# The end of the last block of a gated cross-attention: where x is added, and how the root mean square is formed

## The chip, the cores and the metric

The kernel runs on one core of a Trainium2 chip. A core has a matrix engine (TensorE, PE in the profile, with its weight loads shown apart as PEld), VectorE (DVE), ScalarE (ACT), GpSimd (POOL) and an engine that here only issues transfers (SyncE, SP). Each works through its own list of instructions in order, and they wait for each other by semaphores. Sixteen DMA engines move data between the memory of the chip (HBM) and the core's memory (SBUF). TensorE writes into banks of a small memory of its own, PSUM, which VectorE and ScalarE read.

The metric is the time of one execution in microseconds on the device. The kernel before took 1021.86 us, the median of three runs between 1018.0 and 1022.25.

## The reference

```python
memory_proj = jnp.einsum('bme,de->bmd', memory, W_mem)
scores = jnp.einsum('bnd,bmd->bnm', hidden_states, memory_proj) / jnp.sqrt(jnp.float32(D))
attn = jax.nn.softmax(scores, axis=-1)
memory_context = jnp.einsum('bnm,bmd->bnd', attn, memory_proj)
gate_input = jnp.concatenate([hidden_states, memory_context], axis=-1)
gate = jax.nn.sigmoid(jnp.einsum('bnf,df->bnd', gate_input, W_gate) + b_gate)
fused = hidden_states + gate * memory_context
return _rmsnorm(fused, norm_w)     # x * rsqrt(mean(x*x, -1) + 1e-6) * w
```

Here hidden_states is x, of shape (8, 1024, 1024); memory is (8, 64, 512); the gate has D = 1024 columns. All is in 32-bit floats.

## The kernel before, in words

The 8192 rows of x are worked in 16 blocks of 512 rows, called quads (`q`), two for each batch entry. A quad has four tiles of 128 rows (`t` = 0 to 3); tiles 0 and 1 are row 0 of a two by two scheme, tiles 2 and 3 are row 1. The columns are worked in two halves of 512 (`h`).

The product of x with the upper half of W_gate is made by a fast matrix multiplication in two levels. On the outer level a quad needs seven products, in the order 1, 6, 7, 5, 4, 2, 3 (`ORDER`). Each is again made of seven small ones, which `outer_product` writes in the order A, B, C, D, A (a second part, summed onto the first in the same bank), E, F: two matmuls of 256 columns each. GpSimd forms the sums of x that serve as left operands (`inner_s`), one product ahead. The results are joined by VectorE and GpSimd: ScalarE copies the first part of A (`u<-kA`, line 589) and must have done so before TensorE sums the second part of A onto it; VectorE forms u2, u3, u4 from it with B, C and D; GpSimd adds these to the sums of earlier products (`pre`); VectorE then adds A, D, E and F into the tiles `gate` (`fin`).

Products 5, 4, 2 and 3 each complete a half of two tiles: 5 the second half of row 1, 4 the first half of row 1, 2 the first half of row 0, 3 the second half of row 0. In these (they have an entry `ext` in `ORDER`) TensorE also multiplies the attention weights with the projected memory: once into banks of the gate, once into `pc`, the memory context itself (two buffers, used in turn). ScalarE then takes the sigmoid of the half (line 489), and VectorE multiplies it with `pc` (`gated`, lines 483 to 485). A tile's gating frees its buffer `pc`, which TensorE needs in the next product.

After product 4 (for row 1) and product 3 (for row 0) follow, for each tile:

- `residual` (line 493): a DMA issued by GpSimd that adds x from HBM onto the tile in SBUF,
- `square` (line 503): ScalarE squares the tile, 1024 columns at once, and sums them,
- the root, for two tiles at once (line 508); it needs another table of functions than the sigmoid, loaded by an instruction of its own (ACT_TABLE_LOAD),
- `norm` (lines 514 and 518): VectorE forms the reciprocal and multiplies each half by it and by the weights,
- a store of the whole tile, 512 KB, issued by SP (line 96).

The order is written out by hand. A counter, `slot`, advances with each small product, and `at(slot, f)` puts the instructions of `f` ahead of that small product; `mid` puts them beside the additions of one product. What falls due behind the last product is written out in order of its slots. In most quads squares and norms are spread over the next quad's products; in the last one the norms of row 0 have slots 7 to 10 behind product 3, and those of row 1 keep their usual distance, so that most of row 1's norms are written behind those of row 0. Within an engine instructions keep the order in which they are written. SP's list holds loads and stores alike, so a store that waits for its norm holds what is behind it.

x for a quad's left operands is loaded one quad ahead, in chunks, into four buffers `xqpool`, from which VectorE transposes it (line 267). In the last quad nothing is loaded ahead.

Of the kernel before, what the change touches and what calls it, by code (L numbers as in the profile page):

```python
# [20 lines left out]
def tile_gated_cross_attention_rmsnorm(  # L21
# [70 lines left out]
    def tt(eng, o, a, b, op):  # L92
        pin(eng.tensor_tensor(o, a, b, op))  # L93

    def load(o, i):
        pin(nc.sync.dma_start(o, i))
# [4 lines left out]
    def t4k(pool, shape, tag, name):  # L101
        return pool.tile(shape, F32, tag=tag, name=name)
# [145 lines left out]
    def where(q, t=0):  # L248
        return q // QPB, (q % QPB) * QT + t * P
# [183 lines left out]
    def at(slot, fn, *args):  # L433
        due.setdefault(slot, []).append(lambda: fn(*args))
# [8 lines left out]
    def plan(q):  # L443
        t0 = SLOTS * q
        nxt = q + 1 < NQ
        order = [o for o, _ in ORDER]
        for i, o in enumerate(order):
            for part, t in ((0, 1), (1, 5)):
                if i + 1 < len(order):
                    at(t0 + 7 * i + t, inner_s, q, order[i + 1], part)  # L450
                elif nxt:
                    at(t0 + 7 * i + t, inner_s, q + 1, order[0], part)
        at(t0 + 7, scores, q)
        at(t0 + 7, outer_s, q, 3)
        at(t0 + 7, outer_s, q, 4)
        at(t0 + 9, transpose_scores, q)
        at(t0 + 10, softmax_a, q)
        at(t0 + 13, softmax_b, q)
        at(t0 + 17, transpose_attn, q)
        at(t0 + 20, attn_difference, q)  # L460
        if not nxt:
            return
        for i, t in ((2, 0), (3, 1), (4, 2), (5, 3)):
            at(t0 + i, load_xq, q + 1, t)
        for t in (2, 3):
            mid((q, 5), transpose_x, q + 1, t, 0)
            mid((q, 2), transpose_x, q + 1, t, 1)
        for i, t, half in ((36, 0, 0), (38, 1, 0), (43, 0, 1), (45, 1, 1)):
            at(t0 + i, transpose_x, q + 1, t, half)
        mid((q, 3), outer_s, q + 1, 1)  # L470
        mid((q, 3), outer_s, q + 1, 2)
        if (q + 1) % QPB == 0:
            at(t0 + 10, load_mp, (q + 1) // QPB)
            at(t0 + 49, load_mg, (q + 1) // QPB)
# [35 lines left out]
    def norm(q, t, h):  # L510
        b, n0 = where(q, t)
        rstd = rst[q, t // 2]
        if t % 2 == 0 and h == 0:
            pin(nc.vector.reciprocal(rstd, rstd))
        g = O[q, t]
        cols = slice(h * H, (h + 1) * H)
        pin(
            nc.vector.scalar_tensor_tensor(  # L518
                g[:, cols],
                g[:, cols],  # L520
                rstd[:, t % 2 : t % 2 + 1],
                nw_sb[:, cols],
                ALU.mult,
                ALU.mult,
            )
        )
        if h == 1:
            load(out[b, n0 : n0 + P, :], g)
            del O[q, t]

    def outer_product(q, o, ext):

        nonlocal slot, banks
        l11, l12, l21, l22 = quarters(left(q, o))
        s1, s2, s3, s4 = (L2[q, o][:, i, :, :] for i in range(4))
        w = ws[o]
        kb = {}

        def product(name, tag, lhsT, s, start=True):
            nonlocal slot  # L540
            step()
            if name not in kb:
                kb[name] = ps.tile([P, C], F32, tag=banks[tag], name=f"k{name}{q}_{o}")
            for k in range(2):
                mm(kb[name], lhsT[:, k, :], w[:, s, k, :], start and k == 0, k == 1)
            slot += 1

        def o_blocks(row, h):

            for t in (2 * row, 2 * row + 1):  # L550
                if (q, t) not in O:
                    O[q, t] = t4k(gpool, [P, D], "gate", f"gate{q}_{t}")
            return [
                O[q, 2 * row + r][:, h * H + n * C : h * H + (n + 1) * C]
                for r in range(2)
                for n in range(2)
            ]


        sums = {  # L560
            1: [(o_blocks(0, 0), None)],
            6: [(o_blocks(0, 1), (0, 0))],
            7: [(o_blocks(1, 0), (0, 1))] if o == 7 else [],
            5: [(o_blocks(1, 1), (1, 0)), (o_blocks(0, 1), (0, 1))] if o == 5 else [],
            4: [(o_blocks(1, 0), (1, 0))] if o == 4 else [],
            2: [(o_blocks(0, 0), (0, 0))] if o == 2 else [],
            3: [(o_blocks(0, 1), (0, 1))] if o == 3 else [],
        }[o]
        sums = [(dst, src and o_blocks(*src)) for dst, src in sums]

        def pre(n, u):

            for dst, src in sums:
                if src is not None:
                    tt(nc.gpsimd, dst[n], src[n], u, ALU.add)

        def fin(n, name, u):
            for dst, src in sums:
                if src is not None:
                    tt(nc.vector, dst[n], (src if u is None else dst)[n], kb[name], ALU.add)  # L580
                elif u is not None:
                    tt(nc.vector, dst[n], u, kb[name], ALU.add)
                else:
                    pin(nc.scalar.copy(dst[n], kb[name]))

        ut = t4k(rot, [P, 4, C], "u", f"u{q}_{o}")
        p1, u2, u3, u4 = (ut[:, i, :] for i in range(4))
        product("A", 0, l11, R11)
        pin(nc.scalar.copy(p1, kb["A"]))
        product("B", 1, s2, T2)  # L590
        tt(nc.vector, u2, p1, kb["B"], ALU.add)
        product("C", 2, s3, R12)
        tt(nc.vector, u3, u2, kb["C"], ALU.add)
        pre(3, u3)
        pre(2, u3)
        product("D", 3, s1, T1)
        tt(nc.vector, u4, u2, kb["D"], ALU.add)
        pre(1, u4)
        product("A", 0, l12, R21, False)
        pcs = []  # L600
        if ext:
            row, h, g = ext
            at_, mg = attnTs[q], mgs[q // QPB]
            for n in ("E", "F"):
                kb[n] = ps.tile([P, C], F32, tag=banks[4 if n == "E" else 1], name=f"k{n}{q}_{o}")
            for r, names in ((0, ("A", "F")), (1, ("E", "D"))):
                pc = ps_ctx.tile([P, H], F32, tag="ctx", name=f"pc{q}_{o}_{r}")
                for n in range(2):
                    cols = slice(h * H + n * C, h * H + (n + 1) * C)
                    mm(  # L610
                        pc[:, n * C : (n + 1) * C],
                        at_[0:M, 2 * row + r, :],
                        mg[0:M, cols],
                        n == 0,
                        True,
                    )
                    mm(
                        kb[names[n]],
                        at_[M:P, g + r, :],
                        mg[M:P, cols],  # L620
                        names[n] in "EF",
                        True,
                    )
                pcs.append(pc)
        for fn in beside.pop((q, o), ()):
            fn()
        fin(0, "A", None)
        fin(3, "D", u3)
        product("E", 4, l22, T4, not ext)
        fin(2, "E", u3)  # L630
        if ext:
            sigmoid(q, 2 * row + 1, h)
            at(slot + 1, gated, q, 2 * row + 1, h, pcs[1])
        product("F", 1, s4, R22, not ext)
        fin(1, "F", u4)
        if ext:
            sigmoid(q, 2 * row, h)
            at(slot + 2, gated, q, 2 * row, h, pcs[0])
        if o in (4, 3):

            row = ext[0]
            c, d = 2 * row, 2 * row + 1
            for t in (d, c):
                at(slot + 5, residual, q, t)
            if q + 1 == NQ and row == 0:
                when = (7, 8, 9, 9, 10, 10)
            elif row == 0:
                when = (17, 18, 23, 29, None, None)
            else:
                when = (17, 18, 23, 25, 26, 28)  # L650
            at(slot + when[0], square, q, c)
            at(slot + when[1], square, q, d)
            for w_, (t, h_) in zip(when[2:], ((c, 0), (c, 1), (d, 0), (d, 1))):
                if w_ is None:
                    mid((q + 1, 4), norm, q, t, h_)
                else:
                    at(slot + w_, norm, q, t, h_)
        banks = [banks[i] for i in (2, 3, 0, 4, 1)]
        del L2[q, o]
# [34 lines left out]
```

## Time and profile before

| What | Value |
|---|---|
| median of three runs | 1021.86 us |
| profiled execution | 1022.17 us |
| its span, first to last instruction | 1020.4 us |
| granted TensorE clock, mean | 0.986 |
| TensorE busy | 982.8 us, 96% of the span |
| VectorE busy | 752.8 us, 74% |
| GpSimd busy | 690.5 us, 68% |
| ScalarE busy | 320.2 us, 31% |
| stores `out<-gate`, 64 of 512 KB | 2.6 us from issue to landing (median) |
| `gate<-in_x`, 64 of 512 KB | 7.4 us from issue to landing (median) |

A profile is of one execution. Times in it count from its first instruction. A group row gives the line of the code, engine, operation, output and inputs, their shapes and the count, then busy time in us and the mean in ns, then the idle time ahead of it and what ended most of that. A timeline row gives start and duration in us, and in brackets the idle time before and its releaser. The chain is followed back from the end: at each step to what released it.

### The profile page before, as it was taken

What the parts mean: (1) busy time and instruction counts of PE and PEld (TensorE: products, weight loads), DVE (VectorE), ACT (ScalarE), POOL (GpSimd) and SP (SyncE); (2) the same over time, 40 slices, a digit from 0 to 9 for tenths busy, and PEclk for the clock granted to TensorE, in tenths of its full rate; (3) what the DMA queues carried; (4) which work ended last, traced back from release to release, by engine and by line L of the source; (5) the groups of instructions that cost most, each with busy time, mean ns of one, the idle gap of its engine ahead of it and who ended that gap; (6) DMA issues with size and microseconds to landing.
All of it is one profiled execution on the core that took longest, in us unless ns stands there. A gap on an engine that the chain in (4) does not pass through costs nothing.

```text
span 1020.4 us, 14598 instructions
## 1 busy us (share of the span) xinstructions
PE 982.8 (96%) x4976; PEld 767.9 (75%) x4976; DVE 752.8 (74%) x1464; ACT 320.2 (31%) x587; POOL 690.5 (68%) x855
## 2 busy tenths in 40 slices
PE   7898999999999999999999999999999999999991
PEld 4443687888888887888788888888888878878881
DVE  2065667878878787878787787878787878878763
ACT  0200023334241523333243425142333334341512
POOL 0000477877878787878788787878787878878671
PEclk9899999999999999999999999999999999999996
DMA  7675608164643727192825455372718271543324
GB/s 246 185 187 152 169 1 171 68 140 108 153 106 83 186 76 162 63 187 83 166 73 132 117 131 128 81 188 69 170 62 184 86 165 70 125 128 83 84 72 134
DMA packets 75945, 126.78 MB, mean 124 GB/s; under 512 B 16224, under 2 KB 53088, under 8 KB 75872
## 3 DMA queue, kind: packets, MB, share of 16 engines
q1 hardware_dynamic: 64160, 86.01, 29.0%
q0 software_dynamic: 9216, 33.56, 17.9%
q10 hardware_dynamic: 2496, 6.29, 2.1%
q8 instruction: 39, 0.64, 0.3%
q14 instruction: 34, 0.28, 0.1%
HBM read 85.98 MB, written 39.85 MB: 123 GB/s over the span
## 4 chain that ended last, share of the span: by engine, by line
PE 82%; DVE 12%; DMA 3%; issue 1%; SPq 1%; ACT 0%; ACTq 0%; DVEq 0%; POOL 0%
PE kA L90 17%; PE pc L90 12%; PE kE L90 10%; PE kD L90 8%; PE kF L90 8%; PE kB L90 8%; PE kC L90 7%; PE psT L90 6%; DVE gate L518 5%; PE pm L90 3%; PE pg L90 3%; DVE gate L93 2%; DVE e L93 2%; DVE u L93 1%; DMA gate<-in_x 1%
## 5 line engine op out<-in xcount | busy, mean ns | idle before, releaser
L93 POOL TENSOR_TENSOR gate<-gate,u 128x256 f32<-128x256 f32 x336 | 269.1, 830 | 116.1 <-DVE u L93 92.8
L93 POOL TENSOR_TENSOR l<-a 128x256 f32<-128x256 f32 x128 | 125.5, 980 | 168.3 <-DVE a L267 104.8
L489 ACT ACTIVATE gate<-gate 128x512 f32<-128x512 f32 x128 | 79.3, 630 | 412.1 <-DVE gate L93 412.1
L90 PE MATMUL kA<-ws,a 128*128 128x256 f32 x512 | 131.5, 379 | 0.0
L90 PE MATMUL pc<-mg,attnT 64*128 64x256 f32 x512 | 127.4, 389 | 0.0
L518 DVE SCALAR_TENSOR_TENSOR gate<-gate,ss,nw_sb 128x512 f32<-128x512 f32 x128 | 121.6, 963 | 1.1
L90 PE MATMUL kC<-ws,l 128*128 128x256 f32 x448 | 115.1, 379 | 0.8 <-DVE g L93 0.8
L90 PE MATMUL kD<-ws,l 128*128 128x256 f32 x448 | 115.0, 379 | 0.0
L90 PE MATMUL kB<-ws,l 128*128 128x256 f32 x448 | 115.0, 379 | 0.0
L90 PE MATMUL kF<-ws,l 128*128 128x256 f32 x448 | 115.0, 379 | 0.0
L90 PEld LDWEIGHTS pc<-mg,attnT 64*128 64x128 f32 x512 | 90.6, 186 | 29.8 <-issue 21.2
L90 PEld LDWEIGHTS kA<-ws,a 128*128 128x128 f32 x512 | 97.2, 190 | 13.8 <-DVE s L93 0.2
L90 PE MATMUL kA<-ws,s 128*128 128x256 f32 x384 | 100.2, 383 | 0.0
L90 PEld LDWEIGHTS kB<-ws,l 128*128 128x128 f32 x448 | 85.1, 190 | 11.6
L90 PEld LDWEIGHTS kF<-ws,l 128*128 128x128 f32 x448 | 85.1, 190 | 11.6
L90 PEld LDWEIGHTS kC<-ws,l 128*128 128x128 f32 x448 | 83.8, 190 | 11.8 <-POOL l L93 1.1
L90 PEld LDWEIGHTS kD<-ws,l 128*128 128x128 f32 x448 | 83.9, 190 | 10.7
L93 DVE TENSOR_TENSOR gate<-gate,pc 128x512 f32<-128x512 f32 x128 | 87.1, 681 | 5.3 <-ACT gate L489 5.1
L267 DVE STREAM_TRANSPOSE a<-xq 128x512 f32<-128x512 f32 x128 | 86.0, 693 | 0.0
L93 POOL TENSOR_TENSOR l<-s 128x256 f32<-128x256 f32 x96 | 77.6, 809 | 8.4 <-PE kF L90 5.8
L90 PEld LDWEIGHTS kA<-ws,s 128*128 128x128 f32 x384 | 71.6, 190 | 15.2 <-DVE a L93 6.2
L93 DVE TENSOR_TENSOR u<-u,kB 128x256 f32<-128x256 f32 x112 | 46.8, 418 | 46.3 <-PE kB L90 41.6
(84 smaller groups left out, 1688.0 us busy)
## 6 DMA issues: line engine op xcount, KB each, us to landing
xq<-in_x SPq DMA_DIRECT2D x256, 128.0 KB, 5.5
gate<-in_x POOLq DMA_DIRECT2D x64, 512.0 KB, 7.4
out<-gate SPq DMA_DIRECT2D x64, 512.0 KB, 2.6
w<-in_w_gate_t SPq DMA_DIRECT2D x32, 128.0 KB, 3.3
ws<-in_w_gate_t SPq DMA_DIRECT2D x32, 128.0 KB, 2.9
mg<-mgd SPq DMA_DIRECT2D x8, 512.0 KB, 3.6
wm<-in_w_mem_t SPq DMA_DIRECT2D x4, 512.0 KB, 6.8
mgd<-mp ACTq DMA_DIRECT2D x8, 256.0 KB, 4.4
```

What stands on the lines that cost most here:

```text
L90: pin(nc.tensor.matmul(o, lhsT, rhs, start=start, stop=stop, skip_group_check=True))
L93: pin(eng.tensor_tensor(o, a, b, op))
L267: nc.vector.transpose(A[key][:, :, r * P : (r + 1) * P].rearrange("p j (s c) -> p s j c", c=32), xq[q, t].rearrange("p s (j r) -> p s j r" ...
L489: pin(nc.scalar.activation(g, g, AF.Sigmoid))
L518: nc.vector.scalar_tensor_tensor(g[:, cols], g[:, cols], rstd[:, t % 2 : t % 2 + 1], nw_sb[:, cols], ALU.mult, ALU.mult,)
```

## The change

It touches the last quad alone; the other fifteen are written as before.

- x for the last quad is loaded a second time, by four plain loads on SP of 512 KB (`load_last`), into the buffers `xqpool`. They stand behind the stores of quad 13 and ahead of those of quad 14.
- The accumulating DMAs of GpSimd are left out in that quad. Behind each gating of a half, VectorE adds x of that half (`last_gated`), and ScalarE squares the half and sums it into a column of its own.
- When both halves are there, VectorE adds the two sums, and ScalarE takes the root of one tile (`last_root`).
- `last_norm` forms the reciprocal of a tile, multiplies a half and stores it: 256 KB a store.
- Row 1's roots and norms have slots inside products 2 and 3; row 0's follow product 3.
- In product 3 a root of a constant is written behind the last sigmoid (`sqrt_table`), so that the table is loaded there. Row 1's roots come between the sigmoids of products 4 and 2, so each of them brings a load of its table too.

```diff
         if not nxt:
+            for t in range(4):
+                at(t0 + 5, load_last, t)
             return
...
+    def load_last(t):
+        b, n0 = where(NQ - 1, t)
+        xl[t] = t4k(xqpool, [P, D], "xq", f"xl{t}")
+        load(xl[t], x[b, n0 : n0 + P, :])
+
+    def last_gated(t, h, pc):
+        q = NQ - 1
+        gated(q, t, h, pc)
+        cols = slice(h * H, (h + 1) * H)
+        g = O[q, t][:, cols]
+        tt(nc.vector, g, g, xl[t][:, cols], ALU.add)
+        if t not in halves:
+            halves[t] = t4k(small, [P, 3], f"halves{t}", f"halves{t}")
+        junk = t4k(small, [P, H], "junk", f"junk_{t}_{h}")
+        pin(
+            nc.scalar.activation(junk, g, AF.Square, accum_out=halves[t][:, h : h + 1])
+        )
+
+    def last_root(t):
+        ss = halves[t]
+        tt(nc.vector, ss[:, 2:3], ss[:, 0:1], ss[:, 1:2], ALU.add)
+        pin(nc.scalar.activation(ss[:, 2:3], ss[:, 2:3], AF.Sqrt, bias=eps_sb, scale=1.0 / D))
+
+    def last_norm(t, h):
+        b, n0 = where(NQ - 1, t)
+        rstd = halves[t][:, 2:3]
+        if h == 0:
+            pin(nc.vector.reciprocal(rstd, rstd))
+        cols = slice(h * H, (h + 1) * H)
+        g = O[NQ - 1, t][:, cols]
+        pin(
+            nc.vector.scalar_tensor_tensor(g, g, rstd, nw_sb[:, cols], ALU.mult, ALU.mult)
+        )
+        load(out[b, n0 : n0 + P, cols], g)
+
+    def sqrt_table():
+
+        t = t4k(small, [P, 1], "warm", "warm")
+        pin(nc.scalar.activation(t, eps_sb, AF.Sqrt))
...
+            last = q + 1 == NQ
+            if last:
+                at(slot + 1, last_gated, 2 * row + 1, h, pcs[1])
+            else:
+                at(slot + 1, gated, q, 2 * row + 1, h, pcs[1])
...
+            if last:
+                at(slot + 2, last_gated, 2 * row, h, pcs[0])
+            else:
+                at(slot + 2, gated, q, 2 * row, h, pcs[0])
-        if o in (4, 3):
+        if o in (4, 3) and q + 1 == NQ:
+            c, d = 2 * ext[0], 2 * ext[0] + 1
+            if o == 3:
+                sqrt_table()
+            first = (4, 5) if o == 4 else (3, 3)
+            at(slot + first[0], last_root, d)
+            at(slot + first[1], last_root, c)
+            for i, t in enumerate((d, c)):
+                for h_ in range(2):
+                    at(slot + first[1] + 1 + 2 * i + h_, last_norm, t, h_)
+        elif o in (4, 3):
...
-            if q + 1 == NQ and row == 0:
-                when = (7, 8, 9, 9, 10, 10)
-            elif row == 0:
+            if row == 0:
                 when = (17, 18, 23, 29, None, None)
```

More of the change, by code (lines that the diff above doesn't have):

```diff
@@ L529, in norm @@
             del O[q, t]
+    xl, halves = {}, {}
+    def load_last(t):
[32 more added lines that the diff above has]
+        pin(nc.scalar.activation(t, eps_sb, AF.Sqrt))
     def outer_product(q, o, ext):
@@ L632, in outer_product @@
             sigmoid(q, 2 * row + 1, h)
-            at(slot + 1, gated, q, 2 * row + 1, h, pcs[1])
+            last = q + 1 == NQ
[3 more added lines that the diff above has]
+                at(slot + 1, gated, q, 2 * row + 1, h, pcs[1])
         product("F", 1, s4, R22, not ext)
@@ L637, in outer_product @@
             sigmoid(q, 2 * row, h)
-            at(slot + 2, gated, q, 2 * row, h, pcs[0])
-        if o in (4, 3):
+            if last:
[13 more added lines that the diff above has]
+        elif o in (4, 3):
             row = ext[0]
```

## The prediction

> **What bounds the kernel now.** I began with busy shares: TensorE is busy 96% of the span, so a gain has to come from the stretch in which it isn't, or from its work. The last digits of the forty slices show that stretch: TensorE falls from 9 to 1 in the last slice (25.5 us). The chain that ended last (start and duration in us) says what fills it:
>
> ```profile
> 999.77 0.29 issue
> 1000.06 0.79 POOL gate L493
> 1000.85 7.40 DMA gate<-in_x
> 1008.40 0.90 issue
> 1009.51 1.16 ACT junk L503 x2
> 1010.69 0.30 ACT ss L508
> 1011.22 0.75 DVE gate L518
> 1011.97 0.66 DVEq L690
> 1012.64 3.31 DVE gate L518 x5
> ```
>
> TensorE's last matmul ends at 998.64, the span at 1020.4: 21.8 us of tail, of which 8.2 are the accumulating DMA (POOL issue, transfer), then row 0's squares, root and norms, behind which row 1's norms also stand. The timeline (start, duration) shows how closely the engines follow each other there, and who has time to spare:
>
> ```profile
> 988.97 1.76 POOL L493 DMA_DIRECT2D gate<-in_x  x2
> 990.17 0.63 ACT L489 ACTIVATE gate<-gate 128x512 f32<-128x512 f32 x1 [6.42 <-DVE gate L93]
> 991.57 0.35 ACT L589 COPY u<-kA 128x256 f32<-128x256 f32 x1
> 997.61 1.03 PE L90 MATMUL kF<-ws,l 128*128 128x256 f32 x4
> 999.08 1.47 DVE L93 TENSOR_TENSOR gate<-gate,pc 128x512 f32<-128x512 f32 x2
> 1003.88 0.75 DVE L518 SCALAR_TENSOR_TENSOR gate<-gate,ss,nw_sb 128x512 f32<-128x512 f32 x1
> 1012.66 3.65 SPq L96 DMA_DIRECT2D out<-gate  x4
> ```
>
> Row 1 (tiles 2, 3) is gated by 985.2 and its residual issued at 989, yet one norm apart it ends with row 0. ScalarE idles 6.4 us per product. The fourth line is TensorE's last group, the fifth the last two gatings, the last the four stores of the end. From the groups kept apart by shape (busy us, mean ns of one, idle before), the prices:
>
> ```profile
> L518 DVE SCALAR_TENSOR_TENSOR gate<-gate,ss,nw_sb 128x512 f32<-128x512 f32 x128 | 121.6, 963 | 1.1
> L93 DVE TENSOR_TENSOR ws<-ws 128x512 f32<-128x512 f32 x28 | 17.9, 686 | 0.2
> L503 ACT ACTIVATE junk<-gate 128x1024 f32<-128x1024 f32 x64 | 67.7, 1057 | 5.7 <-DMA gate<-in_x 5.2
> L508 ACT ACT_TABLE_LOAD x31 | 39.8, 1283 | 0.5
> ```
>
> [...] norm takes 0.75 alone, 0.963 in the mean. [...] The trace has the 1.283, but the root follows 0.02 us later (1002.06, 1.28, 1003.36)[...]. [...]
>
> **The change, part by part.** Call the last four products 5, 4, 2, 3, 8.17 us each on TensorE.
>
> Loads of x. They stand in SP's queue behind quad 13's stores, and wait for the last transposes of the tiles they overwrite (936.8 and 938.8). 2 MB at the 200 to 250 GB/s of x loads is in by 950; first needed at 975.4. Queued behind them: quad 14's stores (first norm 955.4), not delayed. They meet quad 14's residuals (issued 933.5 and 945.2; squares at 944.8 and 960.5); each earlier quad loads x there too, and squares waited 0.5 us in all outside the tail. Cost 0; without that cover one or two us in ScalarE's queue.
>
> POOL. Four issues go, 0.88 each, two at 989.0 and two in the tail. POOL has nothing else until its next additions at 993.74, so the first two gain nothing; the other two are in the chain above.
>
> VectorE. Eight adds of 0.69 come in, right after each gating, and row 1's four norms move from the tail into products 2 and 3. In product 3 the sum is: seven 128x256 steps at 0.34 spacing 2.4, two gatings 1.2, two adds 1.4, the norms in it about 2.7, reciprocals 0.4: 8.1 against 8.17 of TensorE. VectorE, which now idles in gaps of 0.3 to 1.1 us there, becomes full[...].
>
> ScalarE. A square with its accumulator read follows the next by 1.17 in the tail (999.73 to 1000.90); a sigmoid of 512 elements takes 0.630 where the square of 1024 takes 1.057, so half the width saves 0.43: 0.74. Each square waits for its add, and behind it in the queue stands the next product's copy u<-kA, which TensorE needs before it writes kA again. This is the wait that the change adds. I lay the instructions of the last products on their engines in queue order, each starting when its engine and its inputs are ready, with the trace's durations (done for before, this ends within 0.15 us of the trace):
>
> Product 4: gating of tile 3 to 975.43, add to 976.1, square to 976.85, copy only then, to 977.2 (before 975.58); u2 at 977.25 (976.31). Gating and add of tile 2 to 978.9, two norms of quad 14 to 982.0 with POOL between (980.14), the four steps of kA to kF after them to 983.4 (982.82). The banks come free in time: no stall. But tile 3's half 0 now gets its sigmoid at 983.08 to 983.71 and its gating at 983.75, 1.0 late.
>
> Product 2: add to 985.26 (POOL in between), square to 986.04, copy 986.04 to 986.40 (was 983.40). TensorE's second kA, due 985.55, starts at 986.44; pc, due 0.95 after it, must wait for the end of tile 2's gating, 987.45. Stall 1.0.
>
> Then square 2 to 988.95, root's table to 990.24, two roots to 990.84, sigmoid's table to 992.13: sigmoids 2 us late, but VectorE has norms of tile 3 to run until 993.1 anyway.
>
> Product 3: gating 993.05, add 994.45, square 995.23, copy to 995.59: second kA, due 994.7, 0.9 late; the norms of tile 2 ahead of tile 0's gating (to 997.32) hold pc another 0.8. Stall 1.7.
>
> Sum: TensorE ends 2.7 later, 998.64 to 1001.3. The trace of before has no such add or half square. Bounds: 0 if copies and gatings fit into the slack (less than nothing can't be, no TensorE work is removed); about 4.5 if adds take 0.95, as norms do in the mean, squares 0.9, and the moved norms meet POOL as often. I take 2.7, the laid-out value.
>
> The tail now (0.08 added, by which the same layout of before ends early): last add kF to 1001.8, sigmoid to 1002.5, root's table to 1003.65, its dummy root to 1003.95, squares of the two last halves to 1005.35 (adds ready 1003.1 and 1004.4, so the table sits in the way for 0.5 to 0.8, but loaded after the squares it would cost 1.2), two roots 0.6 with sums of halves beside them, reciprocals 0.2 each, four norms at 0.67 spacing: last norm ends 1008.9, against 1015.95. Row 1's stores have gone by 997.5.
>
> Stores. Before, four of 0.5 MB fill the end: about 410 GB/s from 1013.4 to 1018.7, 2.7 us past the last norm. Now the last is 256 KB, with nothing queued. A lone 0.5 MB store takes 2.6 from issue to landing; half of 1.28 of transfer less: 1.95. 1008.95 + 1.95 = 1010.9. The end comes about 1.1 after the last landing (1015.98 + 3.3 = 1019.3; 1020.4). Span 1012.0. Half-width rows (2 KB) the trace shows only in other transfers; at half the rate the last piece costs 0.65 more, and a queue of two another 0.65; lower bound 0. I take 0, since the queue has gaps of 0.67 between pieces of 0.64.
>
> So 1020.4 - 1012.0 = 8.4: the tail shrinks from 21.8 to 10.7, 11.1 off, and 2.7 come back through TensorE. The profiled execution took 1022.17, so it would take 1013.8; the median of runs, 1021.86, is 0.3 under it: 1013.5.
>
> **Rivals.**
> No stall: TensorE's slots have slack enough, the 2.7 do not appear: 1010.8. For it: from 948 to 1000 TensorE and its weight loads waited for VectorE 0.2 and 0.4 us only. Against: VectorE's sum in product 3 leaves nothing.
>
> Dear VectorE: [...]4.5 us of stall, and slow half rows: 8.4 - 1.8 - 1.3 = 5.3, 1016.6. For it: two norms took 2.18 at 977.96 against POOL.
>
> Slower: the add's chain is not hidden at all. In products 4, 2 and 3 TensorE would wait at its second kA for sigmoid, gating, add (0.95[...]), square and copy one after the other, 0.63 + 0.68 + 0.95 + 0.74 + 0.36 = 3.4 each, once for two tables and two roots, 3.2, and at pc for two norms in each of products 4 and 3, 4 x 0.96 = 3.8: 17.1 of stall. It decides from 11.1 on, where the tail's gain is used up; 6.0 over gives 1027.9. Against: before, the copy was done 2 us ahead of its use (983.75 for 985.59), and that lead has to be eaten first, in each product.
>
> The x loads don't come early: held on SP until 975, they would stall VectorE; only a wait of 25 us there would do it, and none is in sight.
>
> **How the numbers follow.** Forecast 0.58 (1011.5 to 1015.5), no stall 0.18, dear VectorE 0.20, slower 0.04. This kernel's runs scatter by 4 us, so no change is told from one of less than about 0.5%, 5.1 us: the line is 1016.75. Half of dear VectorE lies beyond it: faster 0.58 + 0.18 + 0.10 = 0.86, same 0.10, slower 0.04. Of the forecast's own span nothing reaches the line. The range runs from the no-stall case less 1.8 for the scatter of medians to the dear case plus 0.9: 1009.0 to 1017.5.
>
> **What would show it.** In the profile after: no POOL gate L493 in quad 15; last matmul near 1001.3; gaps of TensorE of about 1 us in product 2 and 1.7 in product 3, released by ScalarE's copy and a gating; last norm near 1009; the span near 1012. Wrong: TensorE's end at 998.7 (no stall), or beyond 1004; stores queued at the end; ScalarE waiting for x's DMA.

## The result, and the profile after

The changed kernel took 1009.29 us, the median of six runs (1008.79 to 1011.96), against 1019.04 us for the kernel before in the same series (1017.26 to 1022.25). The ratio is 0.9907, with a 95% interval from 0.9884 to 0.9931. A second series gave 1011.86 against 1019.57, ratio 0.9926 (0.9909 to 0.9944). The prediction had said 1013.5 against 1021.86, a ratio of 0.9918.

The profiled execution took 1009.18 us and spans 1007.4. That is 13.0 us less than the profiled execution of before, more than the medians differ, and part of it is no work of the change. It lies at the start. Two stretches there, first of before, then of after (the last three columns are the granted TensorE clock, the share of the DMA engines and GB/s):

```profile
0.00:60.00 60.00, 51.85 (x136) 25.51 (x137) 11.76 (x19) 7.92 (x13) 0.73 (x7) 0.94 0.71 219
60.00:120.00 60.00, 55.46 (x153) 26.62 (x153) 38.64 (x55) 0.74 (x2) 5.65 (x8) 0.97 0.68 173
```

```profile
0.00:60.00 60.00, 51.32 (x144) 25.15 (x145) 13.86 (x22) 7.92 (x13) 0.74 (x7) 0.97 0.73 223
60.00:120.00 60.00, 55.21 (x174) 28.21 (x173) 39.42 (x54) 1.49 (x4) 8.02 (x10) 1.00 0.69 176
```

The clock was 0.94 and 0.97 before, 0.97 and 1.00 after, in code that the change doesn't touch. Product 5 of the last quad starts at 965.80 before and at 960.96 after: 4.84 us were won earlier than any changed product, and all of it is there by the first transpose of x (104.6 us before, 99.8 after). This is scatter: the changed kernel run again starts product 5 at 965.29. The clock goes with it only in part, since the kernel called copies first below, granted 0.997 in the mean of its span where the changed kernel was granted 0.995, starts product 5 at 961.57, later than the changed kernel. What sets the rest is open. From 120 us to the last matmul the clock is 1.00 in both, so I measure every kernel below in two stretches: from the first matmul of product 5 to the end of the last matmul, and from there to the end of the span. Before they are 998.64 - 965.80 = 32.84 and 1020.4 - 998.64 = 21.76, together 54.60. After they are 35.85 and 10.59, together 46.44: 8.16 us less, where the prediction had 8.4.

The chain that ended last, after, in order of time; the accumulating DMA of 7.40 us that stood in it is gone, and VectorE and ScalarE follow each other without a gap of more than 0.04 us (the pieces called issue, which are these gaps, are left out; `warm` is the root of a constant):

```profile
996.91 1.03 DVE gate L93 x2
997.97 1.30 DVE gate L93 x2
999.31 0.20 ACT warm L574
999.51 0.62 ACT junk L551 x2
1000.15 0.72 ACT junk L551 x2
1000.88 0.19 ACT halves L557
1001.10 0.17 DVE halves L563
1001.29 1.42 DVE gate L567 x2
1002.71 0.08 DVE halves L563
1002.82 0.75 DVE gate L567
```

The price stands in the timeline of after. ScalarE's copy (L634) starts behind a square (L551), and TensorE's second kA starts behind the copy:

```profile
980.45 0.63 ACT L551 ACTIVATE junk<-gate 128x512 f32<-128x512 f32 x1 [1.12 <-DVE gate L93]
981.08 0.35 ACT L634 COPY u<-kA 128x256 f32<-128x256 f32 x1
981.49 1.13 PE L90 MATMUL kA<-ws,a 128*128 128x256 f32 x4 [0.36 <-ACT u L634]
...
990.05 0.63 ACT L551 ACTIVATE junk<-gate 128x512 f32<-128x512 f32 x1 [1.42 <-DVE halves L563]
990.68 0.35 ACT L634 COPY u<-kA 128x256 f32<-128x256 f32 x1
991.08 1.13 PE L90 MATMUL kA<-ws,s 128*128 128x256 f32 x4 [1.08 <-ACT u L634]
...
995.78 1.03 PE L90 MATMUL kF<-ws,l 128*128 128x256 f32 x4
```

Product 4 starts at 969.13, product 2 at 977.51, product 3 at 986.39, and its F at 995.78. Against 8.17 a product, and 7.31 from the start of product 3 to its F before (990.30 to 997.61), the stalls are 0.21 in product 4, 0.71 in product 2 and 2.08 in product 3: 3.0 in all.

In product 3 the second kA comes 1.24 us late, behind the copy, and another 0.84 is lost after it. Pieces of the chain show most of that: TensorE's kD starts behind VectorE's additions u3 and u4, and these stand behind a norm (L567), tile 0's gating and the addition of x:

```profile
991.40 0.74 DVE gate L567
992.15 0.61 DVE gate L93
992.78 0.69 DVE gate L93
993.47 0.67 DVE u L93 x2
994.18 0.70 PE kD L90 x2
```

### The profile page after: what moved, and what is told of

Same layout as the page of the kernel before. It is cut to its first block, busy times and chain, and to the rows that moved or that the text cites. A ratio compares the mean times of both kernels' runs of the same rounds, so it can differ in the third digit from the quotient of the medians.

```text
span 1007.4 us, 14639 instructions
## 1 busy us (share of the span) xinstructions
PE 978.7 (97%) x4976; PEld 765.6 (76%) x4976; DVE 760.2 (75%) x1478; ACT 324.7 (32%) x600; POOL 688.0 (68%) x851
## 4 chain that ended last, share of the span: by engine, by line
PE 79%; DVE 14%; DMA 3%; issue 2%; SPq 1%; ACT 1%; ACTq 0%; POOL 0%; DVEq 0%
PE kA L90 16%; PE pc L90 11%; PE kE L90 9%; PE kF L90 8%; PE kD L90 8%; PE kB L90 8%; PE kC L90 7%; PE psT L90 6%; DVE gate L520 4%; DVE gate L93 3%; PE pm L90 2%; PE pg L90 2%; DVE e L93 2%; DVE u L93 1%; DMA mgd<-g 1%
## 5 line engine op out<-in xcount | busy, mean ns | idle before, releaser
L520 DVE SCALAR_TENSOR_TENSOR gate<-gate,ss,nw_sb 128x512 f32<-128x512 f32 x120 | 116.5, 980 | 1.1
L90 PEld LDWEIGHTS kD<-ws,l 128*128 128x128 f32 x448 | 83.9, 190 | 10.7
```

Of the source, the lines that this page charges most:

```text
L90: pin(nc.tensor.matmul(o, lhsT, rhs, start=start, stop=stop, skip_group_check=True))
L520: nc.vector.scalar_tensor_tensor(g[:, cols], g[:, cols], rstd[:, t % 2 : t % 2 + 1], nw_sb[:, cols], ALU.mult, ALU.mult,)
```

## The experiments

All stretches in one table; starts and ends are from the timelines of single profiles, and spans are read to 0.1 us. "Stall" is the first stretch less the 32.84 of before.

| Kernel | product 5 starts | last matmul ends | span | to last matmul | stall | tail | together |
|---|---|---|---|---|---|---|---|
| before | 965.80 | 998.64 | 1020.4 | 32.84 | 0 | 21.76 | 54.60 |
| after | 960.96 | 996.81 | 1007.4 | 35.85 | 3.01 | 10.59 | 46.44 |
| copies first | 961.57 | 995.90 | 1006.4 | 34.33 | 1.49 | 10.50 | 44.83 |
| row 1's norms left out | 964.46 | 999.13 | 1009.7 | 34.67 | 1.83 | 10.57 | 45.24 |
| both of these | 966.26 | 999.33 | 1009.9 | 33.07 | 0.23 | 10.57 | 43.64 |
| copies first, tile 1's root early | 962.10 | 996.43 | 1006.6 | 34.33 | 1.49 | 10.17 | 44.50 |
| no table ahead | 961.53 | 997.36 | 1009.3 | 35.83 | 2.99 | 11.94 | 47.77 |
| loads and adds only | 961.10 | 994.16 | 1011.2 | 33.06 | 0.22 | 17.04 | 50.10 |
| row 0 accumulates | 960.97 | 995.02 | 1015.8 | 34.05 | 1.21 | 20.78 | 54.83 |
| the same again | 960.91 | 994.97 | 1014.7 | 34.06 | 1.22 | 19.73 | 53.79 |
| norms later | 966.32 | 999.38 | 1009.7 | 33.06 | 0.22 | 10.32 | 43.38 |
| after again | 965.29 | 1001.14 | 1011.7 | 35.85 | 3.01 | 10.56 | 46.41 |

### Whose stall is it? Three kernels

The first moves three squares on ScalarE from ahead of the copy to behind it.

```diff
-        junk = t4k(small, [P, H], "junk", f"junk_{t}_{h}")
-        pin(
-            nc.scalar.activation(junk, g, AF.Square, accum_out=halves[t][:, h : h + 1])
-        )
+        if t % 2 == 1 and (t, h) != (1, 1):
+            at(slot + 1, last_square, t, h)
+        else:
+            last_square(t, h)
...
```

> The squares of tiles 3 and 1 that stood ahead of the next product's copy u<-kA on ScalarE are written behind it (three squares move, nothing else). Measured is the stretch from the first kA of product 5 to the end of the last matmul: 32.84 us before, 35.85 after the change, so 3.0 of stall. Theory (two causes, ScalarE's order and VectorE's full queue): the stall falls to about 1.5, the waits of kA for the copy are gone, what is left lies in product 3; the span is 1.5 under the changed kernel's. Rival one (VectorE alone is to blame): the stall stays near 3.0. Rival two (ScalarE's order alone): the stall falls to 0.3 or less.

The stall fell from 3.01 to 1.49. From the tables of waits after the change and with copies first, the rows of TensorE and its weight loads that name another engine (total us, times, longest):

```profile
PEld kA L90 <- ACT u L634: 2.5, 3, 1.5
PE kA L90 <- ACT u L634: 1.4, 2, 1.1
PEld kD L90 <- DVE u L93: 0.4, 1, 0.4
```

```profile
PEld kD L90 <- DVE u L93: 0.7, 1, 0.7
PEld pc L90 <- DVE gate L93: 0.4, 1, 0.4
PE kD L90 <- DVE u L93: 0.3, 1, 0.3
```

The wait for the copy is gone altogether, and waits for VectorE are left: for u4, which frees the bank that kD needs, and a short one for a gating, which frees a `pc`. Both rivals fall, each having said that one cause was all.

The second kernel leaves row 1's norms out (its rows go out unnormalised); the third does both.

```diff
-        pin(
-            nc.vector.scalar_tensor_tensor(g, g, rstd, nw_sb[:, cols], ALU.mult, ALU.mult)
-        )
+        if t < 2:
+            pin(
+                nc.vector.scalar_tensor_tensor(g, g, rstd, nw_sb[:, cols], ALU.mult, ALU.mult)
+            )
```

> The changed kernel without the four multiplications of row 1's norms (left out, their stores kept), which takes 2.9 us of work from VectorE in products 2 and 3. Stretch from product 5 to the last matmul, 3.0 of stall now. Theory (two causes): about 2.2 of stall stay, since the copies still stand behind squares. Rival one (VectorE alone): 0.3 or less. Rival two (ScalarE's order alone): 3.0.

> Both at once: copies ahead of squares, and row 1's norms left out. Theory (two causes): the stall is 0.4 or less, and the tail keeps its 10.6 us from the last matmul on. Both rivals say the same as for the edit that they hold for; if more than 1 us stays, a third cause is at work (the sums of halves or the adds themselves).

Without the norms 1.83 of stall stayed (about 2.2 was expected), with both edits 0.23. So the copies' order is worth 1.52 alone, the norms 1.18 alone, and together 2.78: nearly their sum, two causes of which neither hides the other. The remaining 0.2 is also there with loads and adds only. There all of it lies in product 4, where kD starts at 975.20, just behind u4 (to 975.14), which stands behind two gatings and their additions of x; no run tests this apart.

### The table ahead

```diff
-            if o == 3:
-                sqrt_table()
```

> The changed kernel without the root of a constant behind the last sigmoid: the table is loaded where the root needs it, behind the last squares. Theory: the tail from the last matmul on grows by 1.0 to 1.2 us (10.6 to about 11.7), the stretch from product 5 to the last matmul stays at 35.85. Rival (the table's place is of no matter, as the squares now start as soon as the adds are ready): 0.3 or less.

The tail grew by 1.35 us, a little more than a table load (1.28) and than the 1.0 to 1.2 expected. On ScalarE, in the timeline of this kernel, the load stands right between the last square and the roots:

```profile
1000.63 0.63 ACT L551 ACTIVATE junk<-gate 128x512 f32<-128x512 f32 x1 [0.60 <-DVE halves L93]
1001.16 0.19 ACT L551 ACTIVATION_READ_ACCUMULATOR junk<-gate 128x1 f32 x1
1001.37 1.28 ACT L557 ACT_TABLE_LOAD   x1
1002.66 0.48 ACT L557 ACTIVATE halves<-halves,eps_sb 128x1 f32<-128x1 f32 x2
```

The rival falls. The square of tile 1 starts 0.67 earlier against the last matmul here (999.30 - 997.36 = 1.94) than with the table ahead (999.42 - 996.81 = 2.61), but tile 0's square, which decides, has to wait for its add and starts only 0.07 earlier (3.27 after the last matmul for 3.34).

### Each half of the change alone

First the plain loads and the adds, with squares, roots, norms and whole stores where they had been:

```diff
 # the kernel before; load_last, as in the change, is not shown
         if not nxt:
+            for t in range(4):
+                at(t0 + 5, load_last, t)
             return
...
         tt(nc.vector, g, g, pc, ALU.mult)
+        if q + 1 == NQ:
+            tt(nc.vector, g, g, xl[t][:, h * H : (h + 1) * H], ALU.add)
...
+            if q + 1 < NQ:
                 for t in (d, c):
                     at(slot + 5, residual, q, t)
```

> The kernel before, with only x by plain loads and VectorE's adds in the last quad, no accumulating DMA there; squares of 1024 columns, roots, norms and stores stay where they were. Theory (the DMA is 8.2 us of the tail, but row 1's squares, norms and stores behind it are next in line): the tail from the last matmul on falls from 21.8 to about 17, the stretch from product 5 on grows by about 0.5 (32.84 to 33.3), so some 4 of the 8.2 us are got. Rival (the DMA alone was the matter): the tail falls by 8 us to 13.5. Second rival (the tail is bound by stores of 2 MB at its end): 19 or more.

The tail fell to 17.04, the stretch before it grew by 0.22 (0.5 expected). Both rivals fall. So 4.5 us are won, of the 8.2 that the DMA had held. A part of its chain, again without the pieces called issue, tells where the rest went:

```profile
995.35 1.05 ACT junk L514 x2
996.42 1.15 ACT junk L514 x2
997.58 1.28 ACT L519
998.88 0.29 ACT ss L519
999.17 1.05 ACT junk L514 x2
```

These are row 1's two squares, the root's table and row 1's root, 995.35 to 999.17. Before, these ran from 999.73 to 1003.65, and the DMA from 1000.85 to 1008.25; with the DMA gone, row 0's squares stand behind them. Behind those come seven norms and four whole stores, as before.

Then the other half: row 1 early, as in the changed kernel, row 0 as before, but for the root of a constant, which stays.

```diff
 # the changed kernel
-            for t in range(4):
+            for t in (2, 3):
...
-            last = q + 1 == NQ
+            last = q + 1 == NQ and row == 1
...
-        if o in (4, 3) and q + 1 == NQ:
+        if o == 3 and q + 1 == NQ:
+            sqrt_table()
+        if o == 4 and q + 1 == NQ:
...
-            if row == 0:
+            if q + 1 == NQ:
+                when = (7, 8, 9, 9, 10, 10)
+            elif row == 0:
...
```

> The changed kernel, but row 0 keeps GpSimd's accumulating DMA, squares of 1024 columns, one root and whole stores as before; only row 1 has plain loads, halves and early norms. Theory (row 0's DMA sits at the end of the path whatever row 1 does): the tail is about 18.5 (21.8 less row 1's norms and stores, some 3), the stretch from product 5 on about 1.5 to 2.5 over before, since product 3 has no adds but still the norms; all in all within 2 us of before. Rival (the early work of row 1 is most of the gain): the tail is 14 or less.

> The kernel in which row 0 keeps the accumulating DMA, a second look. Its last transfer took 8.5 us to land where before's took 7.4, and was issued 0.7 later after the last matmul. If that is the transfer's own scatter, the tail is now 19 to 20 (20.8 before); if it is a property of the kernel, it is 20.5 or more again.

The two runs of this kernel give 54.83 and 53.79 together, against 54.60. The rival (early work of row 1 is most of the gain) falls clearly: it had the tail at 14 or less. But my own number for the tail, 18.5, was missed by 2.3 and 1.2, and the stretch ahead of it grew by 1.2 where I had 1.5 to 2.5. Norms and stores did shrink as I had thought: from the reciprocal on, 9.38 before (1011.02 to 1020.4), 6.81 and 6.82 now. What grew is the time from the last matmul to that reciprocal: 12.38 before, 13.97 and 12.91 now. In the chain of the first of these runs the transfer stands longer than the 7.40 of before:

```profile
996.25 0.70 DVE gate L93
997.11 0.58 POOL gate L495
997.70 8.52 DMA gate<-in_x
```

In the other run it landed after 7.5, so this part is the transfer's scatter. The other part was the same in both: GpSimd's first issue comes 2.1 us after the last matmul, where before it came 1.4 after. It follows the end of the second gating of the tail (996.95, above), where before it followed the end of the first (999.77, issue at 1000.06). In both kernels it is written behind both gatings; why it waits for the second one here is open.

The two halves alone gave 4.5 and about 0.3 (-0.2 and 0.8 in its two runs); together they gave 8.16, after paying 3.0 of stall. Each alone leaves the other's work on the path.

### Getting the stall back

Copies first, and the tail's root of tile 1 written ahead of tile 0's last square:

```diff
-            first = (4, 5) if o == 4 else (3, 3)
...
+                at(slot + 2, last_root, d)
+                at(slot + 2, last_square, c, 1)
+                at(slot + 3, last_norm, d, 0)
+                at(slot + 4, last_root, c)
...
```

> Copies ahead of squares as in the first of these, and in the tail tile 1's root and first norm written ahead of tile 0's last square and root. Theory: stall as with copies first, about 1.5; last norm another 0.35 sooner after the last matmul (7.42 after it now, 7.1 then), so the span about 1.9 under the changed kernel's at the same clock. Rival (the tail is bound by VectorE's own gatings and adds): the tail stays at 10.6.

The stall was 1.49 as with copies first, the tail 10.17, 0.33 less: about what was expected, and the rival falls. Its whole time, though, 1008.55, is no less than that of copies first, 1008.28: single runs, and the stretches ahead of product 5 differ by 0.5. It takes the table above to see it.

Then, against the kernel just shown, tile 2's norms, which stood on either side of u2 in product 3, behind u4:

```diff
-                for i, t in enumerate((d, c)):
-                    for h_ in range(2):
-                        at(slot + 6 + 2 * i + h_, last_norm, t, h_)
+                for w_, (t, h_) in zip((6, 7, 11, 13), ((d, 0), (d, 1), (c, 0), (c, 1))):
+                    at(slot + w_, last_norm, t, h_)
```

> Copies ahead of squares, the tail's root of tile 1 first (both as in the runs before this one), and tile 2's two norms written behind u4 of product 3 (one ahead of kA's addition, one ahead of kF's) in place of around u2. Theory (what was left of the stall, 1.49 us, is u3 and u4 of product 3 standing behind these norms): stretch from product 5 to the last matmul 32.9 to 33.2, stall 0.3 or less; tail 10.2 to 10.5. Together 43.2 to 43.6, against 46.44 of the changed kernel and 54.6 of before; ratio to the changed kernel about 0.997. Rival (VectorE is simply full, the order does not matter): stall stays at 1.3 or more.

> The changed kernel once more, timed on the same chip beside the kernel with later norms. Theory: 46.4 us from product 5 to the end again (35.85 and 10.6), since this stretch does not depend on the clock that the set-up at the start is granted; the whole time 8 to 10 us under before. Rival (the profiled execution was a lucky one): the stretch differs by more than 1 us.

The stall is down to 0.22, with all norms made. VectorE is busy for 7.56 of product 3's 8.17 us here (991.04 to 999.21), so it is nearly full, but its work fits in an order in which no u stands behind tile 2's norms. The two norms now fall here:

```profile
996.01 0.42 DVE L93 TENSOR_TENSOR u<-u,kD 128x256 f32<-128x256 f32 x1
996.34 0.16 DVE L570 RECIPROCAL halves<-halves 128x1 f32<-128x1 f32 x1
996.54 0.91 DVE L574 SCALAR_TENSOR_TENSOR gate<-gate,halves,nw_sb 128x512 f32<-128x512 f32 x1
997.37 0.41 DVE L93 TENSOR_TENSOR gate<-gate,kA 128x256 f32<-128x256 f32 x1
...
998.96 0.74 DVE L574 SCALAR_TENSOR_TENSOR gate<-gate,halves,nw_sb 128x512 f32<-128x512 f32 x1
```

The second of them ends 0.3 us behind the last matmul (999.70, for 999.38) and holds up the addition of kF; the tail is 10.32, for 10.17 with tile 2's norms around u2.

This version took 1007.85 us (1005.86 to 1011.7, six runs), the changed kernel in the same series 1011.86 (1009.4 to 1013.49), before 1019.57. The changed kernel is thus 7.71 under before in this series, a little less than the 8 to 10 expected, while its stretch from product 5 on came out again, at 46.41 for 46.44. Against before its ratio is 0.9898 (0.9875 to 0.9921). From product 5 on it takes 43.38, 3.0 less than the changed kernel and 11.2 less than before. This is the shortest of all that were run; the ranges of its runs and the changed kernel's overlap, so the firm number is that of the stretch.

## Why the prediction was right, point by point

Both the size and the two sides of the sum held. The prediction had the tail at 10.7 for 21.8 and TensorE's end 2.7 later; the trace has 10.59 and 3.0. The time alone would not have told this: 1009.29 lies below the forecast's own 1011.5 to 1015.5, nearer to the rival without a stall (1010.8), and only 0.3 above the low end of the whole range, 1009.0. The stretch decides. The stall is there, at 3.0, so that rival falls, and so do the rivals with 4.5 and 17.1 of stall. That the sum of the stalls came so close is in part luck, as its parts show below.

**Loads of x**, counted at nothing: right. They were issued from 926.8 to 934.0, first used at 970.79, and no instruction of VectorE waited for them.

**GpSimd's issues**, nothing in the products and part of the chain in the tail: right as far as tested. Row 0 with the DMA kept puts the old tail back (19.7 and 20.8 for 21.8).

**ScalarE's wait**, the copy behind a square behind an add: shown. It is in the timeline, and moving the squares takes out 1.52 us of the stall.

**VectorE**, called full in product 3: half right. The stall is there (1.18 by leaving the norms out), but the sum of 8.1 us against 8.17 doesn't make it unavoidable. The same work in another order leaves 0.22, with one norm ending 0.3 behind the last matmul. What failed here is the step "VectorE's sum in product 3 leaves nothing"; it was the order that cost, not the sum. The 0.95 for an add of x, with which the rivals of 4.5 and 17.1 reckoned, was an estimate from the mean of a norm (0.963): measured, the eight adds took 0.69 to 0.80, 0.69 in the median.

**The stall's place.** I had 0, 1.0 and 1.7 for products 4, 2 and 3; measured were 0.21, 0.71 and 2.08. Three steps were wrong in detail. Product 4 was to have no stall; there kD starts behind u4, as in the kernel with loads and adds only. In product 3 I held pc until tile 0's gating was over, for 0.8. The trace has pc starting at 992.14 while that gating ran from 992.07 to 992.75, so product 3's first pc does not take the buffer that this gating frees. Its second pc does: with copies first it starts at 991.89, behind that gating's end at 991.83. In its place kD waited for u4, which stood behind the gating, the add and the norm. The copy had been laid out 0.9 late and came 1.24 late; the rest of product 3's stall measured 0.84, close to the 0.8 of a wait that was not there, and that is luck. And the working gave the additions of the sums of halves no time in the products; row 1's took 0.57 and 0.66 in product 2.

**The tail's steps.** Last norm 7.6 after the last matmul (1008.9 less 1001.3), measured 7.42 (1004.23 less 996.81). Stores of 256 KB: 1.95 from issue to landing, measured 2.0 to 2.1; no queue formed at the end. The table in the way for 0.5 to 0.8 us: 0.67; behind the squares 1.2: 1.35.

**The whole time.** The span was forecast at 1012.0 and came out at 1007.4. Of the difference, 4.84 us lie ahead of product 5, and -0.24 in the stretch that the change touches (8.4 less 8.16). The working took the profiled execution's first 960 us as fixed; they aren't (960.96 and 965.29 in two runs of the changed kernel), and that is why the range had to allow for scatter.

## What to carry to other kernels

When work is moved from the end of a kernel into its full part, ask what each engine has queued behind it: a square that waits for VectorE cost 1.5 us because a copy that TensorE needed stood behind it, and nothing but the order had to change to get that back. A transfer that holds the end may hide other work in its shadow, as here 4 of 8 us, so taking it away alone gets only part of it. Compare profiles by the stretch that was changed, with its own start and end, when the rest of the run scatters by more than half of what the change is worth, as here.

## What the runs showed of the hardware that was not expected

An addition of a single column (128x1) on VectorE took 0.16 us in the tail but 0.57 and 0.66 in product 2, while GpSimd was adding:

```profile
983.62 2.10 POOL L93 TENSOR_TENSOR gate<-gate,u 128x256 f32<-128x256 f32 x3 [2.67 <-DVE u L93]
983.79 0.57 DVE L93 TENSOR_TENSOR halves<-halves 128x1 f32<-128x1 f32 x1
985.07 0.66 DVE L93 TENSOR_TENSOR halves<-halves 128x1 f32<-128x1 f32 x1
986.32 1.31 DVE L567 SCALAR_TENSOR_TENSOR gate<-gate,halves,nw_sb 128x512 f32<-128x512 f32 x1
1000.15 0.16 DVE L93 TENSOR_TENSOR halves<-halves 128x1 f32<-128x1 f32 x1 [0.17 <-ACT junk L551]
```

A norm at that place (986.32), beside GpSimd's next sums (985.67 to 987.09), took 1.31 for 0.75. The additions of kA and kD, between the two single columns (984.29 and 984.73) and beside GpSimd's three, took 0.41 and 0.42, as the addition of kF did in the tail (0.42 at 996.91). The second of the single columns in product 2 ends at 985.73, as the last of GpSimd's three does (985.72). With copies first the same addition began at 985.02, 0.13 ahead of the end of GpSimd's three (985.15), and took 0.15. So beside GpSimd a tiny instruction lost here nearly as much as a large one (0.41 and 0.50, against 0.56), and the loss differed with where in GpSimd's work it began. That GpSimd's additions are the cause is read from these times; no run removes them to test it.

The clock granted in the first 120 us differed between executions of code that is the same there: 0.94 and 0.97 before, 0.97 and 1.00 after. In the mean of the whole span the changed kernel was granted 0.995, and 0.990 when run again. In these three executions product 5 of the last quad started at 965.80, 960.96 and 965.29, a scatter of 4.84 us, over half of the 8.16 that the change is worth. The two that started later had the lower clock, but copies first, at 0.997, started product 5 at 961.57, later than the changed kernel at 0.995, so that the clock sets the start is not shown.
